# New durations in the planner that orders a four-layer kernel's instructions

## The chip, the cores and the metric

The kernel runs on one core of one Trainium2 chip. Its time is the device time of one execution in microseconds (us), and the number that counts is the median over several runs. The core has a matrix engine (TensorE, PE in the profile; PEld is its loading of weights), a vector engine (VectorE, DVE), an activation engine (ScalarE, ACT), a general engine (GpSimd, POOL), and SyncE (SP), which here only issues transfers (DMA).

## The reference

Four images of 192 channels and 56 x 56 pixels, in float32, pass through four layers.

- Layer 0: batch normalisation, a 1 x 1 convolution to q, k and v, for each of 6 heads a 7 x 7 convolution from q and k to 49 logits per pixel, a softmax over the 49, and the weighted sum of the 7 x 7 neighbours' v. Then a projection, the residual, and a two-layer perceptron (192 to 768 to 192) with GELU and its residual.
- Layer 1: a gate for each channel, from 7 x 7 pooled sums and a filter chosen from the first image; `x * y + x`.
- Layer 2: layer norm, q, k and v, attention in overlapping 8 x 8 windows at stride 6 with a position bias, the windows folded back and divided by the folded sums; a projection, a high-frequency gate with a depthwise 3 x 3 convolution, the residual; then layer norm and a perceptron in which one half of the hidden channels is normalised, passed through a depthwise 3 x 3 convolution and multiplied into the other half.
- Layer 3: layer norm, a projection to x and z, a depthwise 3 x 3 convolution with SiLU, and four selective scans (rows and columns, both ways) with 4 states for each of 192 channels:

```
h = exp(dt * A) * h + dt * B * u
y = sum over the states of h * C
```

  The four directions are added, normalised, multiplied by silu(z), projected and added to x.

## The kernel before

All four layers are one program. Layers 0 and 1 go by units: one image and a pair of heads, 12 in all. `project` makes q and k; `transform` (VectorE, rows of 868 elements) and `products` (TensorE) are the 7 x 7 convolution in a transformed form, ten products for each unit; `pair` and `ends` add them up on VectorE; `weights` makes the softmax, with its last multiply on GpSimd; `turn_back` and `spread` reorder the weights on TensorE through the one buffer `at_`; `attend` takes the weighted sums of the values that `load` brings; `mlp` is the perceptron by chunks of 448 pixels, and `gate` is layer 1.

Layer 2 has 100 `quad` steps of four windows each: values (line 1873), logits (1893), bias, maximum and exponential (1906 to 1919), transposes (1924), products with the values and with ones (1938, 1951), and the folding (1967). Around them `front` and `back` work on bands of rows, and `head`, `grow` and `tail` on 28 chunks of 8 rows. `dwconv` (1569) is a 3 x 3 convolution on VectorE, `depthwise` (1763) one on TensorE.

Layer 3 has 112 scan steps in two halves, 224 groups. A group takes `du` (2371 or 2374) on VectorE, replicates it on TensorE (2381), multiplies three tiles by B (2387), scans three (2403), multiplies them by C on GpSimd (2410), sums over the states on TensorE (2426) and adds the sum to y (2431, 2436 or 2440). `decay` brings and exponentiates the decays (2356). `begin` and `final` are what stands before and behind the scans.

What sets the order of all this is a planner, the class `Order`. Every piece of work is a generator that yields, ahead of each step, the engine, the step's planned duration and the buffers that it takes. `run` keeps a clock for each engine. Again and again it works out for the first 130 threads when their next step could start: not before the engine is free, the thread's last step has ended (0.25 us after it, 2.5 us after a transfer), the buffers are free, and its conditions hold. It takes the step with the smallest sum of this start and 0.05 us times the thread's place, and only then are the step's instructions written out. TensorE, VectorE, ScalarE and GpSimd carry out their instructions in just this order. SyncE's steps are planned by the same clock at 0.5 us each. The planned durations so decide the order on each engine, the order of the transfers, which of several equal buffers a step takes, and how often ScalarE changes its table of functions; they change nothing in an instruction itself.

The durations come from small helpers (lines 366 to 392). `on_pe` and `on_pe_us` give TensorE's, by 0.0019 us an element or directly; `on_dve` gives VectorE's as a fixed part for each instruction and a part for each element; `on_act` and `on_pool` do the same for ScalarE and GpSimd, `on_scan` for the scans. The steps of layer 3 take theirs from these helpers, with a few slopes of their own.

Of the kernel before, what the change touches and what calls it, by code (L numbers as in the profile page):

```python
# [22 lines left out]
B, C, H, W = 4, 192, 56, 56  # L23
# [8 lines left out]
K49 = WIN * WIN  # L32
# [340 lines left out]


def on_dve(*n, takes=(), ready=None, each=0.00105):
    return "DVE", sum(0.08 + each * i for i in n), takes, None, ready


def on_scan(n, ready):
# [40 lines left out]
def layers01(tc, pools, x_in, packs, aps, dst):  # L420
# [148 lines left out]
    for t in bank_tiles:  # L569
# [3 lines left out]
        bank=bank_tiles,  # L573
# [20 lines left out]
    def begin(b):  # L594

        for c in range(NCHUNK):
            yield on_sp("xc")
            rt = take("xc")
            nc.sync.dma_start(rt[:HALF], pixels(x_in[b])[:, :, c * CH : (c + 1) * CH])
            vt = None  # L600
            for j in range(2):
                yield on_pe_us(1.35, "bank")
                pt = take()
                pv = pt[:112].rearrange("p (i c) -> p i c", i=2)[:, :, :C]
                for i in range(2):
                    for h in range(2):
                        px = 112 * (2 * j + i)
                        nc.tensor.matmul(
                            pv[:, i],
                            rt[:, h, px : px + 112],  # L610
                            w["att.wv"][:, h],
                            start=(h == 0),
                            stop=(h == 1),
                        )
                if j == 1:
                    done(rt)
                yield on_dve(2 * C, takes=() if j else ("vt",))
                if j == 0:
                    vt = take("vt")
                nc.vector.tensor_add(  # L620
                    vt[:, :, 2 * j : 2 * j + 2, :].rearrange("p g i c -> p i g c"),
                    pv.rearrange("p i (g c) -> p i g c", c=64),
                    bcast(v_bias, 1, 2).rearrange("p i (g c) -> p i g c", c=64),
                )
                done(pt)
            if c == 0:
                yield lambda: gone("loads", b - 2)
            for r in range(2):
                yield on_sp()
                nc.sync.dma_start(  # L630
                    vmem[b % 2][:, 3 : 3 + W, r, 4 * c + 2 : 4 * c + 6, :].rearrange("g x y c -> x g (y c)"),
                    vt[56 * r : 56 * r + 56].rearrange("p g i c -> p g (i c)"),
                )
            done(vt)
        passed.add(("v", b))
# [4 lines left out]
    def project(u):  # L640

        b, g = divmod(u, NG)
        yield lambda: gone("projected", u - 1)
        for c in range(7):
            p0, p1_ = 5 * c, min(5 * c + 5, QR)
            spans = [(max(p0, 3), p1_), (p0, min(p1_, 31))]
            yield on_sp("xq")
            xt = take("xq")
            for a, (lo, hi) in enumerate(spans):
                r = lo - 3 + 28 * a  # L650
                nc.sync.dma_start(
                    xt[:HALF, :, a, (lo - p0) * W : (hi - p0) * W], pixels(x_in[b])[:, :, r * W : (r + hi - lo) * W]
                )
            there = order.end + 2.5
            if c == 0:
                yield lambda: gone("transformed", u - 1)
            for i in range(2):
                hd = 2 * g + i
                yield on_pe_us(0.95, "bank", ready=there)
                pt = take()  # L660
                for h in range(2):
                    for a, (lo, hi) in enumerate(spans):
                        s = slice((lo - p0) * W, (hi - p0) * W)
                        nc.tensor.matmul(  # L664
                            pt[halves[a], s],
                            w["att.wqk"][:, h, hd, :],
                            xt[:, h, a, s],
                            start=(h == 0),
                            stop=(h == 1),
                        )  # L670
                if i == 1:
                    done(xt)
                same = spans[0] == spans[1]
                yield on_act(*[280] * (1 if same else 2))
                for a in range(1 if same else 2):
                    lo, hi = spans[a]
                    s = slice(0, 128) if same else halves[a]
                    nc.scalar.activation(  # L678
                        q[s, lo:hi, i, 3 : 3 + W],
                        rows2(pt[s, (lo - p0) * W : (hi - p0) * W]),  # L680
                        AF.Identity,
                        bias=qk_bias[s, hd : hd + 1],
                        scale=qk_scale[s],
                    )
                done(pt)
        passed.add(("projected", u))
# [35 lines left out]
    def products(u, k):  # L722

        yield lambda: (u, k) in made
        yield on_pe_us(4.7, "bank", "bank")
        xt = made.pop((u, k))
        pm = [take(), take()]
        for dx in range(WIN):
            for a in range(2):
                for i in range(2):  # L730
                    nc.tensor.matmul(  # L731
                        pm[a][outs[i], : WIN * W].rearrange("p (y x) -> p y x", x=W),
                        wu[halves[a], k, dx],
                        xt[halves[a], :, i, dx : dx + W],
                        start=(dx == 0),
                        stop=(dx == WIN - 1),
                    )
        done(xt)
        passed.add(("products", u, k))
        return pm  # L740
# [67 lines left out]
    def weights(u):  # L808

        for k, (r0, r1) in enumerate(parts):  # L810
# [1 line left out]
            at = attn[k]  # L812
            n = r1 - r0
            for r in range(0, n, 4):
                yield on_pe_us(0.65, "bank")
                pt = take()
                for i in range(4):
                    nc.tensor.transpose(
                        pt[:112, 128 * i : 128 * i + 128], y[:, r0 + r + i].rearrange("p a x -> p (a x)"), ident
                    )  # L820
                if r0 + r + 4 == 28:
                    passed.add(("turned", u))
                v = pt[:112].rearrange("p (i h k) -> p i h k", i=4, h=2)[:, :, :, :K49]
                yield on_dve(8 * K49)
                mx = p1.tile([112, 4, 2], F32, name="mx", tag=f"mx{r // 4 % 2}")
                nc.vector.tensor_reduce(mx, v, AX.X, ALU.max)
                yield on_dve(8 * K49)
                nc.vector.tensor_sub(at[:112, r : r + 4, :, :K49], v, bcast(mx, 3, K49))
                done(pt)
# [4 lines left out]
            rs = p1.tile([112, n, 2], F32, name="rs", tag=f"rs{k}")  # L834
            nc.vector.tensor_reduce(rs, av, AX.X, ALU.add)
            nc.vector.reciprocal(rs, rs)  # L836
            yield on_pool(2 * n * K49, each=0.0029)
            nc.gpsimd.tensor_mul(av, av, bcast(rs, 3, K49))  # L838
            passed.add(("weights", u, k))

    def turn_back(u):

        for k, (r0, r1) in enumerate(parts):
            yield lambda: gone("weights", u, k) and gone("spread", u - 1)
            for r in range(2):
                for r2 in range(0, (r1 - r0) // 2, 4):
                    n = min(4, (r1 - r0) // 2 - r2)
                    yield on_pe_us(0.2 * n, "bank")
                    pt = take()
                    for i in range(n):  # L850
                        nc.tensor.matmul(
# [17 lines left out]
    def spread(u, a):  # L869
# [1 line left out]
        yield lambda: gone("turned back", u, 1) and (a == 0 or (u, 0) in spread_of)  # L871
        tiles = None
        for c in range(0, 16, 4):
            yield on_pe_us(0.75, "bank", "bank", *(() if c else ("as_", "as_")))
            if c == 0:
                tiles = [take("as_"), take("as_")]
            pk = [take(), take()]
# [49 lines left out]
    def attend(u, a):  # L927
# [9 lines left out]
        for r in range(0, 14, 4):  # L937
            n = min(4, 14 - r)
            yield lambda: (u, a, r) in loads
            v, there = loads[u, a, r]  # L940
            yield on_pe_us(0.45 * n, "bank", ready=there)
            pt = take()
            for bx in range(7):
                for i in range(n):
# [27 lines left out]
    def mlp(b, turn):  # L972
# [3 lines left out]
        for c in range(turn, NCHUNK, 2):  # L976
# [4 lines left out]
            nc.sync.dma_start(xt[:HALF], pixels(x_in[b])[:, :, px])  # L981
            there = order.end + 3
            for h in range(2):
                yield on_pe_us(1.2, "bank", "bank")
                pp = [take(), take()]
                for g in range(NG):
                    for s in range(2):
# [254 lines left out]
def layer2(tc, order, pools, src, packs, aps, dst):  # L1242
# [316 lines left out]
    def dwconv(parts):  # L1559


        for t in range(9):
            yield on_dve(*(n * W for _, _, _, n, _, _ in parts), each=0.0012)
            for dst, pad, i, n, wt, bias in parts:
                x = pad[:, i + t // 3 : i + t // 3 + n, t % 3 : t % 3 + W]
                if t == 0:
# [205 lines left out]
    def tail(i):  # L1772
# [30 lines left out]
        passed.add(("product", i))  # L1803
        px = slice(y0 * W, (y0 + n) * W)
        for h in range(2):
            yield on_pe_us(2.3, "bank", "bank")
            po = [take(), take()]
            hs = slice(HALF * h, HALF * h + HALF)
            for r in range(4):
# [44 lines left out]
    def quad(i):  # L1854
# [3 lines left out]
        yield lambda: at["front"] > j and gone("logits", i - 2)  # L1858

        for z, a in ((xw, xns[j % 2]), (qw, qs[j % 2])):  # L1860
            yield on_pool(256, 256)
            for h in range(2):
                nc.gpsimd.tensor_copy(
                    z[:, h].rearrange("p g w (y x) -> p g w y x", x=WS),
                    strided(strided(window(a[:, h], 0, 0, t), STRIDE * PADW, 2), 5 * STRIDE, 2),
                )

        yield on_pe(4 * C, "bank")
        pt = take()
        pv = pt.rearrange("p (g c) -> p g c", g=2)[:, :, :C]  # L1870
        for g_ in range(2):
# [10 lines left out]
        nc.scalar.copy(v, pv)  # L1882
        done(pt)

        yield on_pe(1200, "bank", "bank", "bank")
        tiles = [take() for _ in range(3)]
        for h in range(2):
            for w_ in range(2):
# [11 lines left out]
        passed.add(("logits", i))  # L1900
        yield lambda: gone("weights", i - 2)

        yield on_dve(320, 320, 320)
        for hd in range(3):
            s = tiles[hd].rearrange("p (h n) -> p h n", h=2)[:, :, :128]
            nc.vector.tensor_add(
# [10 lines left out]
        nc.vector.tensor_sub(ev, ev, bcast(mx, 2, 64))  # L1917
        yield on_act(768, table=EXP_LN)
        nc.scalar.activation(e, e, AF.Exp)
        yield on_pe(6 * 85, "bank", "bank")  # L1920
        tiles = [take() for _ in range(2)]
        for u in range(2):
            for i_ in range(3):
# [5 lines left out]
            nc.scalar.copy(et[:, 3 * u : 3 * u + 3].rearrange("p i n -> p (i n)"), tiles[u][:, :384])  # L1929
            done(tiles[u])  # L1930

        yield on_pe(1500, "bank", "bank")
        tiles = [take() for _ in range(2)]
        os = [x[:HALF].rearrange("p (h j g n) -> p h j g n", h=2, j=2, g=2) for x in tiles]
        for hd in range(3):
# [23 lines left out]
        yield lambda: at["zero"] > j  # L1959
        av = acc.rearrange("p h j y x -> p (h j) y x")  # L1960
        for w_ in range(2):
            yield on_dve(300, 300)
            o = os[w_].rearrange("p h j g (y x) -> p (h j) g y x", x=WS)
            for g_ in range(2):
                y, x = STRIDE * w_, STRIDE * (t + 5 * g_)
# [559 lines left out]
```

## Time and profile before

| | us |
|---|---|
| median of 3 runs | 5724.87 |
| lowest and highest of them | 5719.17, 5725.76 |
| the profiled execution | 5731.28 |
| its span, first to last instruction | 5729.5 |
| TensorE busy | 4866.4 (85%) |
| VectorE busy | 4140.6 (72%) |
| ScalarE busy | 2655.4 (46%), of it 478.6 in 373 loads of tables |
| GpSimd busy | 1699.9 (30%) |

The mean granted clock of TensorE is 0.929 of full speed. The first 143 us collect the statistics of the batch normalisation. Layers 0 and 1 then run to about 2130 us, layer 2 to about 4000, layer 3 to the end; neighbouring layers overlap at the seams.

The views of the profile are read as follows. A group of instructions is one line, engine and operation: its busy time (overlapping records counted once), the mean length of one record, and the engine's idle time just before. A wait is put down to the engine and line whose semaphore came last. The timeline gives start, length and instruction. A TensorE matmul in float32 leaves two records.

### The profile page before, as it was taken

How to read it: one execution, taken by the hardware profiler on the slowest of the kernel's cores; microseconds unless marked ns; L12 is line 12 of the kernel's file. 1: busy time of each engine (PE TensorE's matmuls, PEld its weight loads, DVE VectorE, ACT ScalarE, POOL GpSimd, SP SyncE). 2: the span in 40 equal slices, each digit the busy share in tenths (PEclk: the TensorE clock that was granted, in tenths of full speed). 3: DMA queues.
4: the chain of work that ended last, by engine and by line, in shares of the span. 5: the costliest groups of instructions: out<-in, count | busy, mean ns of one | idle time of the engine just before them, and what ended most of it. 6: DMA issues, size and time to landing. Idle time of an engine off the chain costs nothing. (4 is left out here: it accounts for less than half of the span.)

```text
span 5729.5 us, 137267 instructions
## 1 busy us (share of the span) xinstructions
PE 4866.4 (85%) x58114; PEld 2407.0 (42%) x58114; DVE 4140.6 (72%) x6600; ACT 2655.4 (46%) x4271; POOL 1699.9 (30%) x1688
## 2 busy tenths in 40 slices
PE   4988998998899687898898888868888888888777
PEld 2444554454454444555555555534332232222112
DVE  5788447544744026888988888883678999998997
ACT  0122323212232215555555555546776776676544
POOL 0000000000000013433333433321345555555564
PEclk9999998999999798999999999989998999999998
DMA  6132224333332521000000000002456656566654
GB/s 185 53 80 60 66 60 105 64 88 91 76 69 56 99 77 37 14 22 21 17 22 18 19 20 21 16 26 60 122 135 157 160 145 172 155 149 167 165 149 109
DMA packets 356373, 475.97 MB, mean 83 GB/s; under 512 B 43600, under 2 KB 354256, under 8 KB 355248
## 3 DMA queue, kind: packets, MB, share of 16 engines
q1 hardware_dynamic: 355760, 467.20, 32.9%
q8 instruction: 458, 7.50, 0.5%
q14 instruction: 155, 1.27, 0.1%
HBM read 249.73 MB, written 63.17 MB: 55 GB/s over the span
## 5 line engine op out<-in xcount | busy, mean ns | idle before, releaser
L2410 POOL TENSOR_TENSOR da<-st,bc 128x448 f32<-128x448 f32 x672 | 857.0, 1281 | 751.5 <-DVE st L2403 600.1
L731 PE MATMUL bank<-X,wu 64*49 64x392 f32 x6720 | 610.5, 509 | 89.2 <-DVE X L710 85.9
L2403 DVE TENSOR_TENSOR_SCAN st<-da,st,bank 128x448 f32<-128x448 f32 x576 | 646.3, 1133 | 4.3 <-POOL da L2410 1.8
L838 POOL TENSOR_TENSOR attn<-attn,rs 112x1568 f32<-112x1568 f32 (+1 forms) x24 | 67.1, 2795 | 1726.5 <-DVE rs L836 989.9
L2356 ACT ACTIVATE da<-da,a_neg 128x448 f32<-128x448 f32 x672 | 410.1, 659 | 161.9 <-DMA da<-dt 150.2
L357 ACT ACT_TABLE_LOAD x373 | 478.6, 1283 | 6.6
L2387 DVE TENSOR_TENSOR bank<-bank,bc 128x448 f32<-128x448 f32 x672 | 382.9, 618 | 83.4 <-PE bank L2381 78.2
L731 PEld LDWEIGHTS bank<-X,wu 64*49 64x49 f32 x6720 | 247.6, 123 | 416.1 <-issue 366.4
L2426 PE MATMUL bank<-da,w_c 128*32 128x448 f32 x1344 | 348.8, 575 | 85.3 <-POOL da L2410 66.3
L2381 PE MATMUL bank<-du,w_c 32*128 32x448 f32 x1344 | 291.1, 643 | 105.2 <-DVE du L2371 59.2
L1569 DVE SCALAR_TENSOR_TENSOR bxn<-bapad,w_b,bxn 96x448 f32<-96x448 f32 (+2 forms) x448 | 318.7, 756 | 0.0
L1026 ACT ACTIVATE hm<-bank,w_a 128x448 f32<-128x448 f32 x168 | 106.3, 633 | 435.6 <-PE bank L1017 428.2
L1032 PE MATMUL bank<-hm,w_a 128*96 128x448 f32 x672 | 285.1, 555 | 16.7 <-ACT hm L1026 16.6
L1017 PE MATMUL bank<-xc,w_a 128*128 128x448 f32 x672 | 283.4, 551 | 0.6 <-DVE xc L998 0.6
L1430 POOL TENSOR_TENSOR bsq<-bsq 128x448 f32<-128x448 f32 (+7 forms) x120 | 144.5, 1206 | 446.9 <-ACT bsq L1427 401.8
L678 ACT ACTIVATE q<-bank,qk_bias,qk_scale 128x280 f32<-128x280 f32 (+2 forms) x216 | 116.9, 544 | 294.4 <-PE bank L664 251.2
L2134 PE MATMUL bank<-row,w_c 128*96 128x448 f32 x448 | 206.5, 599 | 29.7 <-DVE row L2100 27.9
L1488 PE MATMUL bank<-bxn,w_b 128*96 128x336 f32 (+2 forms) x576 | 214.3, 498 | 19.0 <-DVE bxn L1440 16.7
L754 ACT COPY sm<-bank 128x392 f32<-128x392 f32 x96 | 43.0, 489 | 380.6 <-PE bank L731 368.2
L2381 PEld LDWEIGHTS bank<-du,w_c 32*128 32x128 f32 x1344 | 92.1, 199 | 299.7 <-DVE du L2371 76.0
L998 DVE SCALAR_TENSOR_TENSOR xc<-bank,w_a,xc 96x224 f32<-96x224 f32 x112 | 44.9, 441 | 226.3 <-PE bank L988 124.5
L1763 PE MATMUL bank<-bzpad,b_diag 32*32 32x224 f32 (+2 forms) x8064 | 182.7, 371 | 24.1 <-ACT bzpad L1735 12.7
(333 smaller groups left out, 10015.4 us busy)
## 6 DMA issues: line engine op xcount, KB each, us to landing
da<-dt SPq DMA_DIRECT2D x672, 224.0 KB
vb<-vmem SPq DMA_DIRECT2D x576, 98.0 KB
bc<-prod SPq DMA_DIRECT2D x224, 224.0 KB
xq<-x SPq DMA_DIRECT2D x132, 210.0 KB
xc<-x SPq DMA_DIRECT2D x56, 336.0 KB
row<-x SPq DMA_DIRECT2D x56, 336.0 KB
xs<-x SPq DMA_DIRECT2D x28, 336.0 KB
vmem<-vt SPq DMA_DIRECT2D x56, 168.0 KB
```

The costliest lines, as they stand in the source:

```text
L357: self.nc.scalar.preload_act_table_set(table)
L731: nc.tensor.matmul(pm[a][outs[i], : WIN * W].rearrange("p (y x) -> p y x", x=W), wu[halves[a], k, dx], xt[halves[a], :, i, dx : dx + W], s ...
L1017: nc.tensor.matmul(ph[:, :CH], w["a128.c1T"][:, k, 128 * m : 128 * m + 128], xt[:, k], start=(k == 0), stop=(k == 1),)
L1032: nc.tensor.matmul(acc[h][:HALF, :CH], w["a128.c2T"][:, m, HALF * h : HALF * h + HALF], hm, start=(m == 0), stop=(m == 5),)
L1488: nc.tensor.matmul(rows2(pq[:HALF, :m]), w["b128." + wn][:, k, HALF * h : HALF * h + HALF], out[:, k], start=(k == 0), stop=(k == 1),)
L1569: nc.vector.scalar_tensor_tensor(dst, x, wt[:, t : t + 1], dst, ALU.mult, ALU.add)
L2356: nc.scalar.activation(da, da, AF.Exp, scale=a_neg[:, k, g : g + 1])
L2381: nc.tensor.matmul(tiles[j][:, :SCH], w["c96.rep"][r], du[r], start=True, stop=True)
L2387: nc.vector.tensor_mul(tiles[j][:, :SCH], tiles[j][:, :SCH], b_)
L2403: nc.vector.tensor_tensor_scan(sts[j][:, r], da[:, r], tiles[j][:, :SCH][:, r], first, ALU.mult, ALU.add)
L2410: nc.gpsimd.tensor_mul(da, sts[j], c_)
L2426: nc.tensor.matmul(py[32 * j : 32 * j + 32, :SCH], w["c128.sum"], das[j], start=True, stop=True)
```

## The change

Durations that steps yield to the planner are replaced, in layers 0 to 2 at their own places, and in all layers through the fixed part of `on_dve`. The instructions stay as they are. The diff:

```diff
 def on_dve(*n, takes=(), ready=None, each=0.00105):
-    return "DVE", sum(0.08 + each * i for i in n), takes, None, ready
+    return "DVE", sum(0.15 + each * i for i in n), takes, None, ready
...
@@ begin, project, products @@
-                yield on_pe_us(1.35, "bank")
+                yield on_pe_us(1.58, "bank")
...
-                yield on_pe_us(0.95, "bank", ready=there)
+                yield on_pe_us(1.1, "bank", ready=there)
...
-        yield on_pe_us(4.7, "bank", "bank")
+        yield on_pe_us(5.05, "bank", "bank")
...
@@ weights, turn_back, spread, attend @@
-                yield on_pe_us(0.65, "bank")
+                yield on_pe_us(0.54, "bank")
...
-            yield on_pool(2 * n * K49, each=0.0029)
+            yield on_pool(2 * n * K49, each=0.0019)
...
-                    yield on_pe_us(0.2 * n, "bank")
+                    yield on_pe_us(0.25 * n, "bank")
...
-            yield on_pe_us(0.75, "bank", "bank", *(() if c else ("as_", "as_")))
+            yield on_pe_us(1.03, "bank", "bank", *(() if c else ("as_", "as_")))
...
-            yield on_pe_us(0.45 * n, "bank", ready=there)
+            yield on_pe_us(0.29 * n, "bank", ready=there)
...
@@ mlp (its projection), dwconv, tail @@
-                yield on_pe_us(1.2, "bank", "bank")
+                yield on_pe_us(1.33, "bank", "bank")
...
-            yield on_dve(*(n * W for _, _, _, n, _, _ in parts), each=0.0012)
+            yield on_dve(*(n * W for _, _, _, n, _, _ in parts), each=0.0013)
...
-            yield on_pe_us(2.3, "bank", "bank")
+            yield on_pe_us(2.4, "bank", "bank")
...
@@ quad: windows, values, logits, bias, transposes, products, folding @@
-            yield on_pool(256, 256)
+            yield on_pool(256, 256, each=0.0015)
...
-        yield on_pe(4 * C, "bank")
+        yield on_pe_us(1.66, "bank")
...
-        yield on_pe(1200, "bank", "bank", "bank")
+        yield on_pe_us(0.9, "bank", "bank", "bank")
...
-        yield on_dve(320, 320, 320)
+        yield on_dve(256, 256, 256)
...
-        yield on_pe(6 * 85, "bank", "bank")
+        yield on_pe_us(0.83, "bank", "bank")
...
-        yield on_pe(1500, "bank", "bank")
+        yield on_pe_us(1.3, "bank", "bank")
...
-            yield on_dve(300, 300)
+            yield on_dve(256, 256)
```

## The prediction

> **What bounds the kernel now.** I read the time stage by stage first, because the planner that the change feeds works on all stages and each has another limit. Busy time of each engine in seven stretches (start and end, length, then PE, PEld, DVE, ACT and POOL busy with their instruction counts, the granted clock, the DMA share, GB/s):
>
> ```profile
> 143.00:1800.00 1657.00, 1522.31 (x19195) 820.46 (x19188) 1007.39 (x1418) 426.40 (x800) 62.05 (x22) 0.96 0.32 73
> 1800.00:2150.00 350.00, 264.44 (x3196) 156.33 (x3196) 72.08 (x141) 82.43 (x154) 33.80 (x22) 0.85 0.38 82
> 2150.00:3700.00 1550.00, 1365.08 (x22347) 815.90 (x22348) 1302.08 (x2617) 858.61 (x1340) 604.78 (x823) 0.93 0.07 21
> 4200.00:5200.00 1000.00, 849.48 (x6301) 279.81 (x6299) 897.14 (x1154) 704.93 (x1097) 546.22 (x447) 0.93 0.61 155
> ```
>
> Layers 0 and 1 (143 to 1800 us) are TensorE's: 92% busy, 135 us idle. Layer 2 (2150 to 3700) is shared: TensorE 88%, VectorE 84%, each waiting for the other in small pieces. Layer 3 (from 4200) is VectorE's: 90%, against TensorE's 85%.
>
> Then the waits of the engine that is the limit in each stage (who waits for whom: total us, times, longest). TensorE in layers 0 and 1, TensorE in layer 2, VectorE in layer 2, and VectorE in layer 3:
>
> ```profile
> PE bank L731 <- DVE X L710: 85.9, 13, 14.8
> ...
> PE bank L1924 <- ACT e L1919: 23.4, 14, 2.9
> ...
> PE bank L1893 <- DVE bzpad L1419: 14.5, 3, 4.8
> PE bank L1893 <- DVE e L1906: 13.2, 10, 3.8
> PE bank L1938 <- ACT et L1929: 10.8, 5, 3.4
> PE bank L1873 <- DVE e L1906: 9.1, 5, 3.3
> ...
> DVE bacc L1967 <- PE bank L1951: 48.2, 22, 5.7
> ...
> DVE e L1906 <- PE bank L1893: 24.5, 15, 10.0
> ...
> DVE bank L2387 <- PE bank L2381: 62.7, 63, 3.2
> ```
>
> The order of instructions is fixed, so each wait is a place where the planned times and the real ones part. Last, the timeline of VectorE, for how long an instruction really holds the engine (start, us, instruction):
>
> ```profile
> 396.26 0.57 DVE L780 SCALAR_TENSOR_TENSOR y<-sm,y 128x392 f32<-128x392 f32 x1
> 396.75 0.56 DVE L780 SCALAR_TENSOR_TENSOR y<-sd,y 128x392 f32<-128x392 f32 x1
> 397.23 0.56 DVE L780 SCALAR_TENSOR_TENSOR y<-sm,y 128x392 f32<-128x392 f32 x1
> ...
> 4618.76 1.67 DVE L2387 TENSOR_TENSOR bank<-bank,bc 128x448 f32<-128x448 f32 x3
> 4620.34 1.14 DVE L2403 TENSOR_TENSOR_SCAN st<-da,st,bank 128x448 f32<-128x448 f32 x1
> 4621.39 0.97 DVE L2374 TENSOR_TENSOR du<-dt,u 96x448 f32<-96x448 f32 x1
> ```
>
> Records of 0.56 us begin 0.48 apart. Three multiplies of 448 elements take 1.67 together, so with a last one of 0.618 (the group's mean) they stand (1.67 - 0.62) / 2 = 0.53 apart; the scan's successor begins 1.05 after it, though its record lasts 1.14. An instruction that needs nothing of its predecessor starts about 0.08 us before that one's record ends.
>
> **The change part by part.** No instruction, tile or transfer is added or removed; only the order within each queue can move, SyncE's included, and which buffer a step takes. So no term is a duration saved: each is a wait that the new order makes or removes. I size them by how far plan and trace stand apart, before and after.
>
> *VectorE's fixed part, 0.08 to 0.15 us, everywhere.* At 448 elements a step is planned at 0.55 before and 0.62 after. The mean record is 0.618, the spacing 0.53. So the old figure is close to what an independent instruction occupies, and the new one is its whole record, which counts the overlap. For a chain (the transform's steps of 868) the new one is nearer: planned 0.99, then 1.06, against 1.12 recorded (L699).
>
> The Trainium skill (VectorE: DVE Perf Modes, The DRAIN you can't avoid) says that after each operation the next does not start until the pipe is empty. By that rule the record is the occupancy, 0.15 is right, and the layer 3 term below would be nothing. The spacings of 0.48 and 0.53 here say otherwise, and I go by them.
>
> *Layer 3.* Nothing else of it is changed. One group (one half of one scan step, 224 in all) has one du, three multiplies, three scans and one addition on VectorE. Planned before: 0.82 + 3 x 0.55 + 3 x 1.13 + 0.55 = 6.41; after 6.76. By the spacings: 0.83 (mean record 0.91 less 0.08) + 3 x 0.53 + 3 x 1.05 + 0.53 = 6.1. The plan thus runs VectorE 5% too long before, 11% after. Between du and the first multiply TensorE replicates du: planned 0.95 with 0.25 of latency on both sides, 1.45 in all, while the three matmuls take 291.1 / 224 = 1.30. The plan fills these 1.45 with other VectorE steps; their real length is 1.45 / 1.05 = 1.38 before and 1.45 / 1.11 = 1.31 after. The lost 0.07 x 224 gives 16 us if each group shows it. The lower bound is nothing (over the whole span 75 of the 224 groups wait here now). What would be late next is the multiply, with three scans queued behind it and GpSimd's multiply behind those. I take 12, nearer the upper end because VectorE is the limit here.
>
> *The window steps of layer 2 (100).* TensorE planned before: values 1.46, logits 2.28, transposes 0.97, products 2.85, in all 7.56; after 1.66 + 0.90 + 0.83 + 1.30 = 4.69. Measured, busy time of the groups over 100: L1873 1.76, L1893 0.87, L1924 0.91, L1938 and L1951 1.56, in all 5.10. So 246 us too much in the plan becomes 41 too little. That cuts both ways. The gain: TensorE arrives at these steps earlier than planned and waits; the rows L1924, L1893, L1938 and L1873 above sum to 71 us, and a plan with the right sizes puts other matmuls ahead. Bounds 0 and 71; I take a third, 24, because half of these waits are on VectorE and ScalarE chains that no size of a matmul shortens. The loss: 2.28 and 2.85 were also margin for the steps that follow on VectorE, L1906 and L1967. They now wait in 15 and 22 of their cases, 1.6 and 2.2 us each. Without the margin (1.30 is planned for 1.56, and the depthwise convolution next to it stays at 0.42 where 182.7 us over 252 steps, 0.72, is measured) I let 15 more of each wait: 15 x 1.6 + 15 x 2.2 = 57. Bounds: none, and all the other cases of one wait for each of 100 steps, 85 x 1.6 + 78 x 2.2 = 308, which the other threads' work must largely hide; the near end is nearer, since 85 and 78 of 100 are hidden today. Net 33.
>
> *The 3 x 3 convolution on VectorE* goes from 0.62 to 0.73 per 448 elements; L1569 averages 0.71 to 0.73. Right, and with the window steps (4.60 to 4.84 planned, 4.53 of records) it makes VectorE the longer engine of layer 2 in the plan, which TensorE is in the trace (1365 against 1302 us). No number of its own: it is in the 57.
>
> *Layers 0 and 1.* Products 4.7 to 5.05 (610.5 / 120 = 5.09 measured), projection 0.95 to 1.1 (1.14), spread 0.75 to 1.03 (1.09), attend 0.45 to 0.29 a row (102.8 us over 96 groups of 3.5 rows: 0.31). All nearer. The 85.9 us of waits for X sit mostly at the change of a unit, where the last projection is followed by seven chained VectorE steps and TensorE has nothing else that is ready; new sizes make no chain shorter. GpSimd's normalisation goes from 4.75 to 3.18 (2.86 in the timeline for the larger part), so the turning back behind it is planned 1.6 earlier, once in each of 12 units: 19 us at most, nothing at least. I take 10.
>
> **The sum.** 12 + 33 - 10 = +35 us. The profiled execution took 5731.28 (span 5729.5, 1.8 around it), 6.4 over the median of the runs, 5724.87. On the median: 5760; on the profiled one 5766.
>
> **The rivals.**
>
> *The better sizes win* (faster). For it: the waits of both engines in layer 2 look like an order made for other lengths, and TensorE's plan error there falls from 246 to 41 us. Against it: margin, and layer 3. Price: 48 of the 71 us go, TensorE wins 10 to 19 in layers 0 and 1 and 15 of its X waits, and the new waits on VectorE stay within 12 and layer 3 at 8: about -58, 5667. It decides if fewer than 5 more of each kind of VectorE wait appear.
>
> *The order hardly matters*: the engines stay as full as they are, gains and losses cancel. For it: 92%, 88% and 90% busy leave little. Price: 5725, 5714 to 5736.
>
> *A bad seam* (slower still). The stretch from 1800 to 2150 has TensorE idle for 86 us, 37.3 of it on loads of vb and 20.6 in one wait for GpSimd at the start of layer 2. An order that moves a load or this first step once more behind a late one doubles these 58: with the 35 and the rest of the seams, about 5830.
>
> **How the numbers follow.** Forecast 0.44, better sizes 0.39, no effect 0.09, bad seam 0.08. The forecast's own range is 5732 to 5795. The range that should hold it 8 times in 10 must take in most of the faster case (5640 to 5712) and the start of the bad seam: 5640 to 5830. What can be told from no change is 0.2%, 11 us. The faster case lies wholly beyond that, 0.39; same is no effect and the first 0.01 of the forecast, 0.10; slower is the rest of the forecast and the bad seam, 0.51.
>
> **What the changed kernel's profile would show.** Instruction counts and record lengths as they are. Right: in the stretch of layer 3 a busy share of VectorE below 90% and more waits of L2387 for L2381 than 63; in layer 2 more than 22 and 15 waits of L1967 and L1906, and less TensorE waiting at L1924, L1893, L1938. Layer 2 longer by about 30 us, layer 3 by about 10, layers 0 and 1 shorter by about 10. Wrong: a layer 2 that ends earlier with TensorE above 90%; or the whole difference in one gap at a seam.

## The result and the profile after

The changed kernel takes 5744.79 us (median of 6 runs, 5738.74 to 5756.9); the kernel before, run beside it, 5723.09 (5718.4 to 5725.76). The ratio is 1.0041, with a 95% interval of 1.0028 to 1.0054: 22 us slower by the medians, where 35 were forecast. The profiled execution took 5745.05 us (span 5743.3), 14 more than the one of before, which lies 8 us above its median.

The 22 us are what is left of larger movements of both signs. These are the ends of a few instructions in the two profiled executions, in us from the start of the span:

| | before | after | moved |
|---|---|---|---|
| last matmul of layer 0's perceptron (L1032) ends | 2127 | 2098 | -29 |
| first folding of layer 2 (L1967) ends | 2193 | 2167 | -26 |
| last folding (L1967) ends | 3756 | 3805 | +49 |
| first scan of layer 3 (L2403) starts | 3989.5 | 4036.5 | +47 |
| last scan ends | 5702 | 5713 | +11 |

Layers 0 and 1 gave 26 us, layer 2 cost 73, and layer 3, from its first scan to the end of the span, gave 33 (1740 to 1707). Three of the stretches that were shown of before are these now (start and end, length, busy PE, PEld, DVE, ACT and POOL with instruction counts, granted clock, DMA share, GB/s):

```profile
143.00:1800.00 1657.00, 1532.05 (x19310) 814.29 (x19303) 1003.34 (x1419) 433.07 (x814) 60.10 (x22) 0.96 0.33 73
...
2150.00:3700.00 1550.00, 1339.33 (x21978) 803.04 (x21976) 1286.81 (x2537) 823.42 (x1284) 603.32 (x792) 0.92 0.07 19
4200.00:5200.00 1000.00, 837.86 (x6394) 271.81 (x6370) 902.76 (x1150) 705.60 (x1095) 546.49 (x448) 0.95 0.61 154
```

In layers 0 and 1 TensorE is busy 10 us more and gets 115 more matmul records done in the same 1657 us. In layer 2 it is the other way: 369 fewer in 1550 us, and both engines are less busy, TensorE by 26 us, VectorE by 15. No engine took over there; both wait more. In layer 3 VectorE goes from 897 to 903 of 1000 us, above 90% rather than below.

The waits of the limiting engines after the change (who waits for whom: total us, times, longest), in the order of before: TensorE in layers 0 and 1, TensorE in layer 2, VectorE in layer 2, VectorE in layer 3:

```profile
PE bank L731 <- DVE X L710: 66.2, 13, 11.2
PE bank L851 <- POOL attn L838: 13.9, 3, 7.0
...
PE bank L1434 <- POOL bsq L1430: 41.0, 21, 5.8
PE bank L1488 <- DVE bxn L1440: 37.2, 16, 4.7
PE bank L1924 <- ACT e L1919: 21.7, 13, 3.3
...
PE bank L1893 <- DVE bacc L1967: 8.2, 6, 5.2
...
PE bank L1938 <- ACT et L1929: 2.1, 5, 0.7
...
DVE bacc L1967 <- PE bank L1951: 60.8, 37, 6.1
...
DVE e L1906 <- PE bank L1893: 28.4, 16, 10.1
...
DVE y L2440 <- PE bank L2426: 33.5, 20, 3.1
DVE bank L2387 <- PE bank L2381: 32.2, 45, 2.0
DVE y L2431 <- PE bank L2426: 21.3, 12, 5.4
```

Three things are to be seen. TensorE waits 20 us less for X. In layer 2 the waits at the window steps did shrink, as the rows of the prediction said they might: the five rows that summed to 71 us sum to 26, though other rows at the same lines grew by some 15. But two waits, at a layer norm and at the projection behind it, grew by 42: L1434 from 19.0 (23 times) to 41.0, L1488 from 16.7 (14 times) to 37.2. And in layer 3, from 4200 us on, the waits of the multiplies for du's copies were halved, 62.7 to 32.2, while the additions' rose, L2440 from 21.9 and L2431 from 2.5.

### The profile page after: what moved, and what is told of

It reads as the page before. It is cut to its first block, busy times and chain, and to the rows that moved or that the text cites. A ratio compares the mean times of both kernels' runs of the same rounds, so it can differ in the third digit from the quotient of the medians.

```text
span 5743.3 us, 137202 instructions
## 1 busy us (share of the span) xinstructions
PE 4839.9 (84%) x58114; PEld 2383.4 (41%) x58114; DVE 4172.2 (73%) x6600; ACT 2647.1 (46%) x4260; POOL 1715.8 (30%) x1688
## 4 chain that ended last, share of the span: by engine, by line
PE 32%; DVE 20%; issue 5%; ACT 3%; POOL 3%; DMA 1%; SPq 0%; POOLq 0%; DVEq 0%; ACTq 0%
DVE st L2403 4%; DVE bxn L1569 4%; DVE bank L2387 3%; PE bank L1664 3%; PE bank L1488 3%; PE bank L2134 2%; PE bank L1763 2%; PE bank L2381 2%; PE bank L2167 2%; PE bank L2426 2%; PE bank L2254 1%; PE bank L1542 1%; PE bank L1812 1%; PE bank L1873 1%; PE bank L1698 1%
## 5 line engine op out<-in xcount | busy, mean ns | idle before, releaser
L731 PE MATMUL bank<-X,wu 64*49 64x392 f32 x6720 | 607.1, 508 | 69.7 <-DVE X L710 66.2
L2403 DVE TENSOR_TENSOR_SCAN st<-da,st,bank 128x448 f32<-128x448 f32 x576 | 647.7, 1135 | 1.6 <-ACT da L2356 1.6
L2426 PE MATMUL bank<-da,w_c 128*32 128x448 f32 x1344 | 370.8, 564 | 101.5 <-POOL da L2410 87.8
L2387 DVE TENSOR_TENSOR bank<-bank,bc 128x448 f32<-128x448 f32 x672 | 383.9, 619 | 46.0 <-PE bank L2381 44.3
L2381 PE MATMUL bank<-du,w_c 32*128 32x448 f32 x1344 | 267.1, 612 | 102.9 <-DVE du L2374 60.6
L1569 DVE SCALAR_TENSOR_TENSOR bxn<-bapad,w_b,bxn 96x448 f32<-96x448 f32 (+2 forms) x448 | 324.3, 765 | 0.0
L1032 PE MATMUL bank<-hm,w_a 128*96 128x448 f32 x672 | 283.0, 551 | 13.0 <-ACT hm L1026 12.9
L1488 PE MATMUL bank<-bxn,w_b 128*96 128x336 f32 (+2 forms) x576 | 220.3, 513 | 41.7 <-DVE bxn L1440 39.0
L2426 PEld LDWEIGHTS bank<-da,w_c 128*32 128x32 f32 x1344 | 60.2, 109 | 383.2 <-POOL da L2410 306.8
L1664 PE MATMUL bank<-bxn,w_b 128*128 128x448 f32 (+2 forms) x448 | 204.3, 581 | 5.0 <-DVE bxn L1440 3.3
L699 DVE SCALAR_TENSOR_TENSOR X<-q 128x868 f32<-128x868 f32 x72 | 81.1, 1126 | 171.3 <-ACT q L678 107.1
```

Of the source, the lines that this page charges most:

```text
L731: nc.tensor.matmul(pm[a][outs[i], : WIN * W].rearrange("p (y x) -> p y x", x=W), wu[halves[a], k, dx], xt[halves[a], :, i, dx : dx + W], s ...
L1488: nc.tensor.matmul(rows2(pq[:HALF, :m]), w["b128." + wn][:, k, HALF * h : HALF * h + HALF], out[:, k], start=(k == 0), stop=(k == 1),)
L1569: nc.vector.scalar_tensor_tensor(dst, x, wt[:, t : t + 1], dst, ALU.mult, ALU.add)
L1664: nc.tensor.matmul(tiles[u][:, : n * W], w["b128.fc1T"][:, k, 128 * m : 128 * m + 128], xn[:, k, : n * W], start=(k == 0), stop=(k == 1),)
L2381: nc.tensor.matmul(tiles[j][:, :SCH], w["c96.rep"][r], du[r], start=True, stop=True)
L2387: nc.vector.tensor_mul(tiles[j][:, :SCH], tiles[j][:, :SCH], b_)
```

## The experiments

All variants give `on_dve` its fixed part by layer, so that one layer's durations can be changed alone. With 0.08 three times the durations are those of before; each diff below shows what differs from that. The lines of a variant stand 5 to 11 further down in the file than those of the two kernels.

```diff
-def on_dve(*n, takes=(), ready=None, each=0.00105):
-    return "DVE", sum(0.08 + each * i for i in n), takes, None, ready
+def on_dve(*n, takes=(), ready=None, each=0.00105, fixed=0.08):
+    return "DVE", sum(fixed + each * i for i in n), takes, None, ready
+
+DVE01 = functools.partial(on_dve, fixed=0.08)   # on_dve of layers 0 and 1
+DVE2 = functools.partial(on_dve, fixed=0.08)    # of layer 2
+DVE3 = functools.partial(on_dve, fixed=0.08)    # of layer 3
```

All results at a glance; each ratio is against runs of the kernel before on the same chip, with its 95% interval. The difference is that of the medians.

| run | what is new in it | ratio | interval | us |
|---|---|---|---|---|
| only01 | layers 0 and 1, all | 0.9968 | 0.9957-0.9979 | -18 |
| only2 | layer 2, all | 1.0132 | 1.0117-1.0147 | +74 |
| only3 | layer 3 (fixed part 0.15) | 0.9965 | 0.9954-0.9976 | -21 |
| both01and3 | layers 0, 1 and 3 | 0.9932 | 0.9918-0.9947 | -40 |
| l2vector | layer 2, VectorE and GpSimd only | 1.0074 | 1.0059-1.0089 | +43 |
| l2margin | layer 2, all but logits and products | 1.0103 | 1.0086-1.0120 | +62 |
| l2nofixed | layer 2, all but the fixed part | 1.0074 | 1.0059-1.0089 | +43 |
| l2tiny | layer 2, fixed part 0.085 and nothing else | 1.0070 | 1.0055-1.0085 | +38 |
| l3overlap | layer 3, engine free 0.08 before the record's end | 1.0085 | 1.0070-1.0100 | +51 |
| l3ten | layer 3, fixed part 0.10 | 0.9997 | 0.9987-1.0007 | -3 |
| l3sixteen | layer 3, fixed part 0.16 | 0.9928 | 0.9911-0.9945 | -36 |
| l3long | layer 3, fixed part 0.22 | 1.0025 | 1.0015-1.0036 | +9 |

### Which layer, and do the layers add up?

only01, only2 and only3 take the change apart by layers; both01and3 leaves layer 2 alone.

```diff
 # only01
+DVE01 = functools.partial(on_dve, fixed=0.15)
-                yield on_pe_us(1.35, "bank")
+                yield on_pe_us(1.58, "bank")
...
-                yield on_pe_us(1.2, "bank", "bank")
+                yield on_pe_us(1.33, "bank", "bank")
```

> New durations in layers 0 and 1 alone (steps and VectorE's fixed part), the old ones in layers 2 and 3. In the profile of the full change the last perceptron matmul of these layers ends at 2096 instead of 2121 us. Theory A, each layer's own durations decide its own time and the three add: 25 us less, about 5698. Theory B, the layers' orders are tied together and what one wins the seam behind it gives back: 5715 to 5730, with layer 2 starting earlier and ending where it ended.

```diff
 # only2
+DVE2 = functools.partial(on_dve, fixed=0.15)
-            yield on_dve(*(n * W for _, _, _, n, _, _ in parts), each=0.0012)
+            yield on_dve(*(n * W for _, _, _, n, _, _ in parts), each=0.0013)
...
-            yield on_dve(300, 300)
+            yield on_dve(256, 256)
```

> New durations in layer 2 alone. In the full change layer 2 took 73 us longer (its last folding moved from 3756 to 3805 although it began 25 earlier). Theory A, it is layer 2's own durations: about 5723 + 73 = 5796, or some 5780 if a part is taken back at the seam to layer 3. Theory B, layer 2 fell out of its steady pattern because layers 0 and 1 handed over at another moment: 5715 to 5740.

```diff
 # only3
+DVE3 = functools.partial(on_dve, fixed=0.15)
```

> VectorE's fixed part 0.15 in layer 3 alone, all else old. In the full change layer 3 took 33 us less from its first scan to the end, where my prediction had 12 more. Theory A, the longer fixed part itself makes the better order in layer 3: about 5690. Theory B, the gain came from the other moment at which layer 3 began or from TensorE's clock, and the fixed part costs what I predicted: 5723 to 5735.

```diff
 # both01and3: the edits of only01 and only3 together
+DVE01 = functools.partial(on_dve, fixed=0.15)
+DVE3 = functools.partial(on_dve, fixed=0.15)
-                yield on_pe_us(1.35, "bank")
+                yield on_pe_us(1.58, "bank")
...
```

> New durations in layers 0, 1 and 3, the old ones in layer 2. Theory A, the parts add: 5723 - 25 - 33 = 5665. Theory B, the parts do not add: 5700 to 5730.

Measured: 5698.7, 5791.46, 5695.89 and 5676.95 us, beside 5717.11 for the kernel before. So layers 0 and 1 and layer 3 each gain, layer 2 loses more than both, and the stages add up: 0.9968 x 0.9965 = 0.9933 against 0.9932 measured for the two together, and with 1.0132 all three come to 1.0064, with a half-width of 0.0022 from the three intervals, against 1.0041 +/- 0.0013. The seams between layers need no term of their own that these intervals could show. The four came out as theory A of each had them, but for both01and3, 12 us above its 5665: that was added up from the 25 and 33 us of a single pair of profiles, where the medians of only01 and only3 give 18 and 21. (The ends that the expectation of only01 gives as 2121 and 2096 are the 2127 and 2098 of the table.) both01and3 is faster than the kernel before and than the changed one.

### Layer 2: is it the lost margin?

The prediction put the loss of layer 2 on the margin that the old durations of logits and products (2.28 and 2.85 us) gave the steps behind them. l2vector leaves all of TensorE's old durations, l2margin only those two, and l2nofixed takes everything but the fixed part.

```diff
 # l2vector: TensorE's durations stay
+DVE2 = functools.partial(on_dve, fixed=0.15)
-            yield on_dve(*(n * W for _, _, _, n, _, _ in parts), each=0.0012)
+            yield on_dve(*(n * W for _, _, _, n, _, _ in parts), each=0.0013)
-            yield on_pool(256, 256)
+            yield on_pool(256, 256, each=0.0015)
-        yield on_dve(320, 320, 320)
+        yield on_dve(256, 256, 256)
-            yield on_dve(300, 300)
+            yield on_dve(256, 256)
```

> In layer 2 only VectorE's and GpSimd's new durations (fixed part 0.15, the convolution's slope, 256 elements for bias and folding, the window copies); TensorE's steps keep the old ones, so logits 2.28 and products 2.85 keep their margin. Layer 2 alone with all of its new durations cost 74 us. Theory M, the lost margin on TensorE costs it: nearly nothing remains, 5705 to 5735. Theory V, VectorE planned too long costs it: 5770 to 5800.

```diff
 # l2margin: as only2, but these two stay
         yield on_pe(1200, "bank", "bank", "bank")
...
         yield on_pe(1500, "bank", "bank")
```

> All new durations in layer 2 but for the logits and the products of a window step, which keep 2.28 and 2.85. Theory M: as l2vector, 5705 to 5735, since these two carry the margin. Theory V: 5770 to 5800.

```diff
 # l2nofixed: as only2, but
+DVE2 = functools.partial(on_dve, fixed=0.08)
```

> All new durations in layer 2 but for VectorE's fixed part, which stays 0.08. Theory M: the loss stays, 5770 to 5800. Theory V: it goes, 5705 to 5735.

Measured: +43, +62 and +43. With all the margin still there l2vector loses 43, where the margin theory (M) had nearly nothing; with the margin of the two steps given back l2margin still loses 62 of 74. In that form the margin theory falls; a small part, such as the 12 us, can't be told from one order or another. That VectorE is planned too long (V) falls too, since without its longer fixed part l2nofixed still loses 43; l2vector and l2nofixed lie between the ranges of both theories. What is left is odd: whichever part of the change is taken out, some 40 us or more stay lost, as if any change at all lost them. Nor do they lose it in one place: in l2nofixed the time from the first folding to the last is only 18 us longer than before, and the time from there to the first scan 32 us (266 against 233). TensorE's new durations alone were not tried, since with these the planner finds no order: it runs out of free buffers.

### Layer 2: any change at all

The time from the end of one image's last window step to that of the next is 420, 420 and 415 us in the kernel before. In every run whose layer 2 durations are the old ones it is the same three numbers; in the others it is 396, 475 and 425 (after), 394, 475 and 425 (only2), 443, 441 and 398 (l2vector), 434, 430 and 438 (l2margin), 455, 425 and 396 (l2nofixed). That led to a theory of another kind: under the old durations the planner had fallen into an order that repeats from image to image, and any other number throws it out. l2tiny adds 5 ns to VectorE's fixed part, 1% of a 448-element step and far less than the 0.07 by which the plan of such a step and its mean record part, and changes nothing else.

```diff
 # l2tiny
+DVE2 = functools.partial(on_dve, fixed=0.085)
```

> VectorE's fixed part in layer 2 goes from 0.08 to 0.085 us, all else as before: a change of 5 ns per instruction, well inside what separates plan and trace. In the profile before, the VectorE order of layer 2 repeats exactly from image to image, every 420 us; in each variant with other layer 2 durations it doesn't repeat, and each lost 42 to 74 us. Theory C, the old durations had led the planner into a repeating cycle that happens to be good, and any other number leaves it: 5745 to 5790. Theory S, it is the size of the durations that counts: 5710 to 5730.

Measured: 5758.57 against 5720.7, +38. The 5 ns cost half of what all of the new durations of layer 2 cost. Here are the stretches between those ends, the columns as above. Two of the kernel before:

```profile
2501.00:2921.00 420.00, 376.07 (x6216) 222.63 (x6214) 360.69 (x724) 235.38 (x364) 164.71 (x218) 0.94 0.07 19
2921.00:3341.00 420.00, 375.75 (x6216) 222.54 (x6214) 361.42 (x724) 235.50 (x364) 161.69 (x218) 0.94 0.07 19
```

All three of the changed kernel:

```profile
2508.00:2905.00 397.00, 348.16 (x5715) 209.28 (x5712) 334.43 (x657) 220.86 (x340) 157.11 (x200) 0.94 0.07 19
2905.00:3380.00 475.00, 410.17 (x6643) 240.59 (x6644) 401.09 (x789) 246.01 (x383) 184.99 (x237) 0.91 0.07 19
3380.00:3805.00 425.00, 357.58 (x5858) 209.89 (x5868) 352.64 (x703) 227.12 (x343) 145.05 (x189) 0.88 0.06 18
```

And of l2tiny:

```profile
2517.00:2934.00 417.00, 367.50 (x6134) 217.80 (x6130) 360.08 (x714) 228.61 (x356) 168.05 (x206) 0.94 0.07 19
2934.00:3377.00 443.00, 386.24 (x6300) 227.68 (x6301) 373.40 (x735) 232.07 (x362) 170.89 (x230) 0.93 0.07 19
3377.00:3804.00 427.00, 368.24 (x6093) 218.53 (x6093) 359.27 (x711) 231.83 (x351) 157.28 (x191) 0.92 0.06 18
```

In the kernel before the two stretches hold the same number of instructions on every engine (6216, 724, 364, 218) and the same busy time within 1 us on TensorE, VectorE and ScalarE; the instructions stand in the same order on each engine. After and in l2tiny no two stretches are alike, 657 to 789 VectorE instructions in one. So that the 5 ns break the repetition and cost 38 us is shown. That the repetition itself is what makes the old order good is not: it may be one good draw that happens to repeat. The changed kernel's 397 us is no counterexample, since it holds fewer instructions and VectorE is busy for 84% of it, against 86% of the 420; but the last such stretch of l2vector, whose order does not repeat, has VectorE at 87% (346 of 397 us). Of the 73 us that layer 2 costs after, the three stretches hold 41 (1255 to 1296), and the first image's window steps, which stand ahead of them, 33 (2193 to 2501 before, 2167 to 2508 after). One rival was not tested: the granted clock is 0.91 and 0.88 in the last two stretches of the changed kernel, 0.94 and 0.93 before. Whether that costs time, or only follows from TensorE's waits, no run here tells; in l2tiny it is 0.94 to 0.92, and 38 us are lost all the same.

### Layer 3: is the truer figure the better one?

only3 gains 21 us by planning each VectorE step 0.07 longer. One theory (R) says that a figure nearer what the trace shows orders better; a second (E), that the longer VectorE is planned here the better; a third (C), that it is a draw, as in layer 2. l3overlap follows the spacings of the trace: a result counts as ready at the end of the record, and the engine as free 0.08 earlier.

```diff
 # l3overlap
-            self.engines[engine] = self.end
+            self.engines[engine] = self.end - (0.08 if engine == "DVE" and th[5] == "3" else 0.0)
...
+def DVE3(*n, takes=(), ready=None, each=0.00105):
+    return "DVE", 0.08 + sum(0.07 + each * i for i in n), takes, None, ready
```

> Layer 3 alone is changed: the planner lets a VectorE step hand on its result at the end of its record (one 0.15 per step), but holds the engine 0.08 us less, as the spacing of the records shows. The plain 0.15 in layer 3 won 21 us. Theory R, the gain came from handing on results at the true time: the gain stays or grows, 5680 to 5700. Theory E, the gain came from VectorE planned longer than it is, which leaves room for TensorE's steps that take longer than planned: the gain goes, 5712 to 5730.

```diff
 # l3long
+DVE3 = functools.partial(on_dve, fixed=0.22)
```

> VectorE's fixed part in layer 3 is 0.22, far longer than any record; all else as before. So far, held by spacing 5770, 0.08 5719, 0.15 5696. Theory E, a VectorE that is planned longer makes the better order in layer 3: 5680 to 5700. Theory R, the true end of the record is what helped: 0.22 is as far from it as 0.08, 5710 to 5730. Theory C, chance: anything from 5690 to 5770.

```diff
 # l3ten
+DVE3 = functools.partial(on_dve, fixed=0.10)
```

> VectorE's fixed part in layer 3 is 0.10, between the old and the new; all else as before. Theory E and theory R: between 5696 and 5719. Theory C, chance: outside of these two by 10 us or more.

```diff
 # l3sixteen
+DVE3 = functools.partial(on_dve, fixed=0.16)
```

> VectorE's fixed part in layer 3 is 0.16, 10 ns more than the 0.15 that won 21 us; all else as before. Theory R, a plan whose VectorE steps end where the records end makes the better order: 5690 to 5706, as 0.15. Theory C, 0.15 hit a good order by chance: back to 5711 or more, or another 10 us faster than 0.15.

Measured: 5770.39 (+51), 5729.84 (+9), 5718.12 (-3, within the interval of no change) and 5686.49 (-36). The form nearest to the spacings is the slowest of all, outside the ranges of both R and E. It says less about R than it seems, because VectorE's own work grew in it. From the end of the first scan to that of the last VectorE is idle for 194 us, 209 before, but busy for 1559, 1502 before. The `du` multiplies account for that: all of them together take 264.5 us against 203.4. Here is one of their two lines, before and then in l3overlap, where it is L2385 (busy us, mean ns, idle before):

```profile
L2374 DVE TENSOR_TENSOR du<-dt,u 96x448 f32<-96x448 f32 x112 | 108.8, 971 | 0.0
```

```profile
L2385 DVE TENSOR_TENSOR du<-dt,u 96x448 f32<-96x448 f32 x112 | 156.9, 1400 | 0.0
```

The last section shows when a `du` is long: when a GpSimd instruction is under way as it starts. That is so for 127 of the 224 in l3overlap and for 27 before. The granted clock fell as well, from 0.92 to 0.88 between the same two scans, so the 61 us of `du` are not shown to be the whole cause.

Longer than the record loses again at 0.22, where E had 5680 to 5700; E falls. Along the fixed part the time goes 0, -3, -21, -36, +9 for 0.08, 0.10, 0.15, 0.16 and 0.22. The two beside the record's own length are the good ones, but 10 ns between them are worth 15 us (the two intervals do not overlap). l3sixteen came out 4 us below what R gave as its limit, and met the sign that C had named, another 10 us or more faster than 0.15. Whether the record's length helps because it is true, or two orders out of many happen to be good, stays open. The edits of only01 with 0.16 in layer 3, which by the ratios would be the fastest here, were not run together.

Where only3 gains can be read image by image: from the end of the first scan to that of the 168th, 336th, 504th and 672nd. This pair of profiles lies 33 us apart, the medians 21. First the kernel before, then only3, the columns as above:

```profile
3991.00:4477.00 486.00, 415.70 (x3344) 144.57 (x3346) 375.52 (x481) 339.06 (x528) 225.72 (x193) 0.89 0.54 137
4477.00:4894.00 417.00, 354.68 (x2624) 117.35 (x2619) 379.34 (x490) 293.70 (x456) 231.68 (x191) 0.94 0.62 158
4894.00:5313.00 419.00, 354.64 (x2632) 117.67 (x2631) 380.27 (x490) 291.99 (x456) 230.95 (x190) 0.94 0.62 158
5313.00:5702.00 389.00, 286.33 (x901) 68.98 (x900) 366.92 (x479) 192.72 (x284) 231.30 (x176) 0.91 0.57 149
```

```profile
3987.00:4445.00 458.00, 400.53 (x3350) 138.76 (x3348) 377.89 (x483) 328.05 (x520) 225.78 (x192) 0.95 0.58 148
4445.00:4868.00 423.00, 353.28 (x2632) 114.93 (x2632) 384.75 (x491) 296.42 (x458) 231.97 (x191) 0.95 0.61 156
4868.00:5294.00 426.00, 355.11 (x2632) 115.56 (x2632) 384.54 (x490) 296.48 (x458) 231.72 (x191) 0.95 0.60 155
5294.00:5666.00 372.00, 268.45 (x883) 65.61 (x882) 365.30 (x477) 193.33 (x281) 229.46 (x176) 0.97 0.59 154
```

The two middle images lengthen, by 6 and 7 us. The first and the last shorten, by 28 and 17. In the last one VectorE was idle for 389 - 367 = 22 us and is now for 7; in the first, for 110 and now 80. The gain is idle time of VectorE at the two ends of the stage, where the four images do not overlap as they do in the middle. The granted clock rises there too, 0.89 to 0.95 and 0.91 to 0.97; over the whole kernel it was 0.938 to 0.942 in all 7 runs of only3 and 0.929 to 0.934 in the 16 runs of before beside them, so it is no accident of one run. Whether it is a cause or follows from the other order, no run here tells.

## Why the prediction was right and wrong

**Direction and size.** Slower was forecast, by 35 us, and 22 were measured. But the sum came near by luck: all three terms were off, layer 2 by 41 us one way, layers 0 and 1 by 8 and layer 3 by 33 the other. That has to be told term by term.

**Layers 0 and 1 (-10).** Right in sign; only01 measured -18, and the first folding ends 26 us earlier after. The place was wrong. The prediction held that new sizes make no chain shorter and let the 85.9 us of waits for X stand; they are 66.2 now. How they got shorter was not taken apart: the chain of VectorE steps ahead of X is the same. The gain expected from the turning back did not show: its wait for GpSimd grew from 8.0 to 13.9. Which of the durations brings the gain was not taken apart, nor whether a meaningless small change would have brought as much.

**Layer 2 (+33 net).** Right in sign, less than half in size: only2 measured +74. The gain of 24 came: of the rows that sum to 71, L1938 went from 10.8 to 2.1, and the waits of L1893 and L1873 for the step at L1906 are no longer among the longer ones; with the new rows at these lines some 30 us are gone. The loss term failed. It expected more waits at L1967 and L1906, 57 us of them; they went from 48.2 to 60.8 and from 24.5 to 28.4, 16 in all, with the 15 more cases forecast at L1967 and 1 at L1906, and giving back the margin to logits and products (l2margin) won only 12 of the 74. The waits that grew on TensorE, L1434 and L1488, are at a layer norm and at the projection behind it, which the working did not look at. The step that failed is the method: it let better and worse come from how far plan and trace stand apart, while the order before was lost by every other set of numbers tried in layer 2, all six, l2tiny's 5 ns among them. (The 0.71 to 0.73 read for L1569 is 0.74 for the records of 448 elements; no term hangs on it.)

**Layer 3 (+12).** Wrong: only3 measured -21. The fill argument spoke of the steady images, and these did lengthen, by 6 and 7 us in only3, about the size it gave. But not by its mechanism: L2387 waits 32.2 us after against 62.7 before, where more than 63 cases were predicted there are 45, and VectorE's own work grew by 10 us in these two images, in only3 as in the changed kernel, where 7 of them are the longer `du` of the last section; "record lengths as they are" did not hold. What the step left out was the ends, the first and the last image, where VectorE had 110 and 22 us idle and where a new order could gain. The share of 90% was read from 4200 to 5200 us, which leaves out the last image and much of the first.

**VectorE's fixed part.** The reading that an independent step starts 0.08 us before its predecessor's record ends holds in the changed kernel's records as well. That the planner is better off with the spacing does not follow: l3overlap lost 51 us, though its `du` records alone grew by 61, so it is no clean trial of the spacing.
The Trainium skill's rule that was weighed (VectorE: DVE Perf Modes, The DRAIN you can't avoid) has, at the end of the paragraph, a sentence that the prediction left out, that an instruction which is not held starts earlier; with that sentence the page and the spacings of 0.48 and 0.53 agree, and the rule speaks no more against the term than for it.

**The rivals.** "Better sizes win" had the right sign for layers 0 and 1; in layer 3 it priced a loss of 8 where only3 won 21. Its condition in layer 2, fewer than 5 more cases of each kind of VectorE wait, was not met at L1967 (15 more). "The order hardly matters" falls: 5 ns in the plan move the time by 38 us, though gains and losses did cancel in part. The bad seam did not come: in the stretch around it TensorE waits 45.6 us for loads of vb, 37.3 before, and 20.8 at the start of layer 2, 20.6 before; neither doubled.

## What to carry to other kernels

Where a list scheduler fixes the order, its durations are knobs of a search and not only a model: here 5 ns on one number cost half of what all the new numbers of layer 2 cost, so change them stage by stage, measure each stage, and keep the good ones (here layers 0, 1 and 3, -40 us). Before an order that seems to be made of wrong numbers is redone, look whether it repeats from one item to the next; a repeating order has the same instruction counts in each stretch, and here 5 ns were enough to lose it. Look whether the new order makes any instruction itself longer. And look at the first and last item of a stage by themselves: here the idle time that could be won of the limiting engine sat there.

## What the runs showed of the hardware

One VectorE instruction depends on what GpSimd does. `du` at L2371 multiplies two tiles that lie in SBUF. In the two middle images it is slower in the changed kernel, 970 ns on average against 845, for 56 instructions each. The first group line is of the kernel before, the second of the one after (busy us, mean ns, idle before):

```profile
L2371 DVE TENSOR_TENSOR du<-dt,u 96x448 f32<-96x448 f32 x56 | 47.3, 845 | 0.0
```

```profile
L2371 DVE TENSOR_TENSOR du<-dt,u 96x448 f32<-96x448 f32 x56 | 54.3, 970 | 0.0
```

That is 7 of the 10 us by which VectorE is busier in these two images after. The single records lie between 0.59 and 2.59 us before (median 0.596). The timeline of the changed kernel has both kinds (start, length, instruction, and in brackets the idle time before it); VectorE first, then GpSimd in the same stretch:

```profile
4510.75 1.13 DVE L2403 TENSOR_TENSOR_SCAN st<-da,st,bank 128x448 f32<-128x448 f32 x1
4511.81 2.53 DVE L2371 TENSOR_TENSOR du<-dt,u 96x448 f32<-96x448 f32 x1
...
4532.15 0.60 DVE L2371 TENSOR_TENSOR du<-dt,u 96x448 f32<-96x448 f32 x1
```

```profile
4510.69 2.07 POOL L2245 TENSOR_TENSOR row<-row,gate 96x896 f32<-96x896 f32 x1 [0.16 <-ACT row L2237]
4512.73 1.13 POOL L2410 TENSOR_TENSOR da<-st,bc 128x448 f32<-128x448 f32 x1
...
4532.37 1.37 POOL L2410 TENSOR_TENSOR da<-st,bc 128x448 f32<-128x448 f32 x1 [5.47 <-ACT dt L2322]
```

The long one begins while GpSimd runs a multiply, a second follows without a gap, and `du` ends at 4514.34, 0.48 us after the second (4513.86), about as if it had begun only then. Where `du` begins first, it keeps its 0.60 us, and the GpSimd multiply that starts under it takes 1.37 instead of 1.13. The multiply at L2387, with one input in PSUM, has a mean of 618 ns before and 619 after.

The pattern holds over the whole kernel before. Of the 112 `du` at L2371, 85 start with no GpSimd instruction under way and take 0.59 to 0.62 us. The other 27 start under one and take 1.63 on average, and 24 of them end 0.48 us after the end of a GpSimd instruction.

The Trainium skill says of this (SBUF — State Buffer, Who interferes with whom) that a VectorE instruction with two SBUF inputs contends with a GpSimd instruction that reads SBUF, for an exclusive lock, and that the order of issue decides which of them waits. These records agree, with one thing more: the long `du` waited for two GpSimd instructions in a row. No experiment here isolated it; l3overlap, which moved more `du` under GpSimd's work, also changed the rest of layer 3's order.
